# The last image's last queries in three blocks, and its last two involution units in parts ordered by row

## The chip, the cores and the metric

The kernel runs on one core of one Trainium2 chip. The metric is device time in microseconds (us), as the median of several runs; before the change it is 2607.41 us.

## The reference

The input is four images of 512 channels and 64x64 pixels, float32. Two layers follow each other:

- Attention. With N = 4096 pixels and 128 inner channels, `q`, `k` and `v` are 1x1 convolutions of `x`; `out[:, i] = sum_j v[:, j] * softmax_j(q_i . k_j)`; a 1x1 convolution `wo` brings it back to 512 channels, and `x` is added.
- Involution. `o1 = relu(W1 x)` has 128 channels in 8 groups of 16. For each pixel a small network (`Wr`, relu, `Ws`) makes 7x7 weights per group, `w[g, dy, dx]`. The output at a pixel is the sum over the 49 neighbours of `w[g, dy, dx] * o1[c, y + dy - 3, x + dx - 3]`, with zeros outside of the image. A 1x1 convolution `W3` brings it back to 512 channels, and the layer's input is added.

## The kernel before

**Attention.** The images go one after the other (`b`), the queries of an image in chunks of 512 pixels, that is eight rows (`c`, 0 to 7). `attention` runs steps: a step makes the scores of one block of queries against 128 keys (`pss`), ScalarE takes their exponential (`pt`), TensorE multiplies by `v` into `po`, and VectorE adds `pt` into `pacc`, whose last addition is `sums`. A block has `n` queries; with fewer than 512, one `pss` tile of 512 columns holds `512/n` keys' blocks. In the last image the last chunk is two blocks of 256 (blocks 7 and 8, here the image's rows 56 to 59 and 60 to 63).

**Finishing a block** (`finish_block`): `sums` is reduced (`blocks`), multiplied by `quads` (`pl`), inverted (`rls`), spread to all partitions (`spread`), multiplied into `on`; then `pwo` (four matmuls with additions into `x` on VectorE), `p1`, the relu `o1`, a transpose `pp`, a copy `o1t`, a DMA to a padded image `pix` in DRAM, and `pr` with its relu `red`, from which the taps' weights come.

**Involution.** A unit `u` is four image rows (16 units an image). It lies as two tiles `t` of 128 pixels, two rows each. `weights` makes `pw` (2 x 392 columns of PSUM) from `red`. The rows with their seven shifted windows are loaded from `pix` to `ring`, which has 12 slots for rows (`pump`, on SyncE's queue, three rows a piece at most in the last image). A VectorE instruction multiplies `n` values of `dy` for one shift `x` and both tiles: `prod <- ring, pw`, with 2 x `n` x 128 elements in a partition. `dy` goes in (0..3) and (4..6), cut into two where the rows would wrap in the ring. The products are summed over `x` and `dy` by GpSimd (`acc <- acc, prod`) and, in the tail, every second one by TensorE, with the product as stationary matrix and an identity as moving one (`pa`). `prods` has four buffers, so a product waits for the summing of the one four before it.

**Closing a unit** (`turn_unit`, `close_chunk`): TensorE adds `acc` to `pa`, ScalarE copies it (`accT`), and four matmuls `py` with four VectorE additions and the output DMA follow.

**Order.** Python generators are interleaved while the program is written: attention's steps drive, and `chores` steps the finishing, the closing and the products (`taps`), the latter by a planner's own times (`pe`, `free`, `due`). After the last attention step comes the tail: `tail` is set, the planner's waits fall away, a second PSUM pool for `pw` takes the place of the scores' (`wpools` then holds two, used in turn), and the loop steps finishing, closing and taps in turn until all is done. Within an engine's queue the order of the built program stands.

When a unit of the tail reaches `dy` 4, the kernel also makes the next unit's weights ahead:

```
                if o and dy >= DYS[1][0] > ops[o - 1][1]:
                    low = base + UR
                    pump()
                    if tail and units:
                        early[units[0]] = weights(*units[0])
...
            pw = early.pop((b, u), None) or weights(b, u)
```

The lines of the profile: products L356, GpSimd's sums L380, every matmul through `mm` L220 (told apart by tile), `sums` L699, `blocks` L537, the additions after `pwo` L560, after `py` L461, `pp` L590, `accT` L446, the ring's loads L257.

Of the kernel before, what the change touches and what calls it, by code (L numbers as in the profile page):

```python
# [8 lines left out]
F32 = mybir.dt.float32  # L9
AF = mybir.ActivationFunctionType  # L10
ALU = mybir.AluOpType
AX = mybir.AxisListType

B, C, H, W = 4, 512, 64, 64
N = H * W
P = 128
CT = C // P
CH = 512
NCH = N // CH
# [4 lines left out]
K = 7  # L24
PAD = 3
NTAP = K * K
GC = 16
G = P // GC
# [8 lines left out]
O_WP = 6 * 512  # L37
# [10 lines left out]
V_SP, V_BP = V_BVC + 1, V_BVC + 2  # L48
NVEC = V_BVC + 3

UR = 4
NT = UR // 2
NU = H // UR
# [3 lines left out]
RING = 12  # L57
STEP = 72
SR = UR + K - 2

DYS = (0, 4), (4, 3)
TAPS_A_US = 1.56


# [19 lines left out]
def fast_path(  # L84
# [91 lines left out]
    def takes(engine, us):  # L176
        free[engine] = max(free[engine], pe) + us
        return free[engine]
# [33 lines left out]
    def w_slice(off, t):  # L212
        return wt[:, off + t * P : off + (t + 1) * P]

    def v1(i):
        return vec[:, i : i + 1]

    def mm(o, lhsT, rhs, start=True, stop=True, shared=1):
        pe_us(rhs.free_size() * PE_COLUMN / shared)
        return nc.tensor.matmul(o, lhsT=lhsT, rhs=rhs, start=start, stop=stop)  # L220
# [19 lines left out]
    def pump():  # L240

        nonlocal load
        while load // STEP in written:
            b, row = divmod(load, STEP)
            rows, us = written[b]

            end = H + SR - UR if rows == H else rows + PAD - 1
            n = min(b * STEP + end, low + RING) - load
            n = min(n, RING - load % RING, PIECE if b == B - 1 else RING)
            if n <= 0:  # L250
                break
            for h in range(2):
                src = pix[b % 2][row + h : row + h + n, :W, :]
                windows = bass.AP(
                    tensor=src.tensor, offset=src.offset, ap=[[P, W], [WP * P, n], [1, K * P]]
                )
                nc.sync.dma_start(  # L257
                    ring[h * W : (h + 1) * W, load % RING : load % RING + n]
                    .rearrange("p r x c -> p r (x c)"),
                    windows,  # L260
                )
            free["dma"] = max(free["dma"], us)
            us = takes("dma", ROW_US * n) + LAND_US
            landing.update((load + i, us) for i in range(n))
            load += n
            if row + n == H + SR - UR:
                load = (b + 1) * STEP
# [4 lines left out]
        pace()  # L272


    def weights(b, u):
        red, col = reds[b, u]
        wpools.append(wpools.pop(0))
        pw = wpools[0].tile([P, NT, CH], F32, tag="w", name=f"pw_{b}_{u}")
        for t in range(NT):

            rows = slice(t * (P // NT), t * (P // NT) + CR + 1)
            pixels = slice(col, col + P)
            mm(
                pw[:, t, : NTAP * G], red[rows, pixels], wt[rows, O_WT : O_WT + NTAP * G],
                shared=2,
            )
        return pw
# [15 lines left out]
        nc.vector.tensor_scalar(verdict, pn, P - 0.5, None, ALU.is_lt)  # L303


    def involution():
        nonlocal low, due
        while True:
            while not units:
                yield "none"  # L310
            b, u = units.pop(0)
            acc = work2.tile([P, NT, 4, P], F32, tag="acc", name=f"acc_{b}_{u}")
            yield from until(free["dve"] + 0.3)
            pw = early.pop((b, u), None) or weights(b, u)
            begin = pe + 0.5
            pa, ops = None, []
            base = b * STEP + u * UR
            for dy0, n in DYS:

                at = (base + dy0) % RING  # L320
                whole = at + n + NT < RING + 1
                pieces = [(dy0, n)] if whole else [(dy0, 2), (dy0 + 2, n - 2)]
                ops += [(x, dy, k) for x in range(K) for dy, k in pieces]
            for o, (x, dy, n) in enumerate(ops):
# [5 lines that stand above are left out]
                rows = [(base + dy + t * 2) % RING for t in range(NT)]  # L330
                while base + dy + n + NT > load:
                    yield "wait"
                landed = max(landing[base + dy + i] for i in range(n + NT))
                while not tail and (
                    pe < max(begin, landed)
                    or free["dve"] > pe + (4.5 if b == B - 1 else 3.5)
                    or free["pool"] > pe + lag
                ):
                    yield "wait"
                free["pool"] = max(free["pool"], takes("dve", DVE_TAPS[0] + DVE_TAPS[1] * n))  # L340
                takes("pool", POOL_TAPS[0] + POOL_TAPS[1] * n)
                due -= n
                d0 = dy - DYS[dy >= DYS[1][0]][0]
                first = x == 0 and dy < DYS[1][0]
                prod, p0 = acc, d0
                if not first:
                    prod, p0 = prods.tile(
                        [P, NT, 4, P], F32, tag="prod", name=f"prod_{b}_{u}_{o}"
                    ), 0
                col = (x * K + dy) * G  # L350
                lines = ring[:, rows[0] : rows[0] + n, x, :]
                image = bass.AP(
                    tensor=lines.tensor, offset=lines.offset,
                    ap=[lines.ap[0], [(rows[1] - rows[0]) * K * P, NT], [K * P, n], [1, P]],
                )
                product = nc.vector.tensor_tensor(  # L356
                    prod[:, :, p0 : p0 + n, :].rearrange("p t d (g c) -> p t d g c", g=G),
                    image.rearrange("p t d (g c) -> p t d g c", g=G),
                    pw[:, :, col : col + n * G].unsqueeze(3)
                    .broadcast_to([P, NT, n * G, GC])  # L360
                    .rearrange("p t (d g) c -> p t d g c", d=n),
                    ALU.mult,
                )
                if not tail:
                    tc.keep_in_program_order(product)
                if first:
                    pass
                elif tail and o % 2:

                    begun = pa is not None  # L370
                    if not begun:
                        pa = ps1.tile([P, NT, P], F32, tag=("po", "acc")[u % 2], name=f"pa_{b}_{u}")
                    for t in range(NT):
                        for d in range(n):
                            mm(
                                pa[:, t, :], prod[:, t, d, :], ident,
                                not begun and t == d == 0, False,
                            )
                else:
                    nc.gpsimd.tensor_tensor(  # L380
                        acc[:, :, d0 : d0 + n, :], acc[:, :, d0 : d0 + n, :], prod[:, :, :n, :],
                        ALU.add,
                    )
                yield
            low = max(low, (b + 1) * STEP if u == NU - 1 else base + UR)
            pump()
            if pa is None:
                for n in (2, 1):
                    nc.gpsimd.tensor_tensor(  # L389
                        acc[:, :, :n, :], acc[:, :, :n, :], acc[:, :, n : 2 * n, :], ALU.add  # L390
                    )
            closing.append(turn_unit(b, u, acc, pa, takes("pool", POOL_OP * 1.5)))
# [127 lines left out]
    def finish_block(b, c, off, n, po, sums):  # L520
# [97 lines left out]
                    )  # L618
        us = takes("dma", PIX_US) + LAND_US

        pr = ps.tile([P, CH // NT], F32, tag="mm", name=f"pr_{name}")[:, : n // NT]
        for t in range(NT):
            half = slice(t * (P // NT), (t + 1) * (P // NT))
            mm(
                pr[half], w_slice(O_WP, 0)[:, half],
                o1.rearrange("p (u t x) -> p u t x", t=NT, x=P)[:, :, t, :], shared=2,
            )
        red = redpool.tile([P, CH // NT], F32, tag="red", name=f"red_{name}")[:, : n // NT]
        nc.scalar.activation(red, pr, AF.Relu, bias=v1(V_BP), scale=v1(V_SP))
        for i in range(tiles // NT):  # L630
            reds[b, top // UR + i] = red, i * P

        rows = top + n // W
        written[b] = rows, us
# [12 lines left out]
    def attention(b, kt, vT, q):  # L647
        blocks = [(c, 0, CH) for c in range(NCH)]
        if b == B - 1:

            blocks[-1:] = [(NCH - 1, off, CH // 2) for off in (0, CH // 2)]

        steps = [(k, j) for k, (_, _, n) in enumerate(blocks) for j in range(N // P * n // CH)]
        qs, pts, pos, paccs = {}, {}, {}, {}
# [470 lines left out]
```

## Time and profile before

| what | value |
|---|---|
| runs | 2607.64, 2607.41, 2604.98 us; median 2607.41 us |
| profiled execution, first to last instruction | 2605.7 us |
| median less the profiled span | 1.7 us |
| TensorE busy | 2587.9 us (99%) |
| VectorE busy | 1874.2 us (72%) |
| GpSimd busy | 1823.5 us (70%) |
| ScalarE busy | 835.8 us (32%) |
| mean granted TensorE clock | 0.997 |
| last exponential of the attention (`pt`) starts | 2522.82 us |

No other time of the profiled execution is given than its span; the median stands 1.7 us above it, for what lies around the instructions and for the spread of the runs. Start and duration in a line of the trace are microseconds from the span's start. A bracket behind a line of the timeline is the idle time of that engine before it, and what ended it. TensorE's rows count two instructions for one float32 matmul.

### The profile page before, as it was taken

What the parts mean: (1) busy time and instruction counts of PE and PEld (TensorE: products, weight loads), DVE (VectorE), ACT (ScalarE), POOL (GpSimd) and SP (SyncE); (2) the same over time, 40 slices, a digit from 0 to 9 for tenths busy, and PEclk for the clock granted to TensorE, in tenths of its full rate; (3) what the DMA queues carried; (4) which work ended last, traced back from release to release, by engine and by line L of the source; (5) the groups of instructions that cost most, each with busy time, mean ns of one, the idle gap of its engine ahead of it and who ended that gap; (6) DMA issues with size and microseconds to landing.
All of it is one profiled execution on the core that took longest, in us unless ns stands there. A gap on an engine that the chain in (4) does not pass through costs nothing.

```text
span 2605.7 us, 24569 instructions
## 1 busy us (share of the span) xinstructions
PE 2587.9 (99%) x7484; PEld 1246.5 (48%) x7484; DVE 1874.2 (72%) x2677; ACT 835.8 (32%) x1378; POOL 1823.5 (70%) x1197
## 2 busy tenths in 40 slices
PE   9999999999999999999999999999999999999998
PEld 7444444445544444444644444444464444444577
DVE  0447777877575787788676678788757678777887
ACT  1333333332233333333223333333323333333330
POOL 0007788877881788887885468888788577877886
PEclk9999999999999999999999999999999999999999
DMA  6033232445615344233651434443463433222343
GB/s 236 1 75 63 55 85 73 99 99 150 164 43 112 63 101 95 61 84 82 180 129 45 103 69 101 101 92 74 118 171 83 101 93 93 72 60 58 73 91 102
DMA packets 208798, 244.33 MB, mean 94 GB/s; under 512 B 109640, under 2 KB 128528, under 8 KB 208528
## 3 DMA queue, kind: packets, MB, share of 16 engines
q1 hardware_dynamic: 208224, 242.31, 38.6%
q8 instruction: 61, 1.00, 0.2%
q14 instruction: 81, 0.66, 0.1%
q10 hardware_dynamic: 432, 0.36, 0.0%
HBM read 193.57 MB, written 49.06 MB: 93 GB/s over the span
## 4 chain that ended last, share of the span: by engine, by line
PE 91%; POOL 4%; DVE 3%; issue 1%; DMA 0%; ACT 0%; SPq 0%; POOLq 0%; DVEq 0%; ACTq 0%
PE pss L220 32%; PE po L220 31%; PE pv L220 4%; PE pk L220 4%; PE pq L220 4%; PE pwo L220 4%; PE py L220 4%; PE p L220 4%; POOL acc L380 4%; PE pw L220 2%; DVE prod L356 1%; PE pa L220 1%; DVE pacc L696 1%; PE pr L220 1%; POOL acc L389 0%
## 5 line engine op out<-in xcount | busy, mean ns | idle before, releaser
L380 POOL TENSOR_TENSOR acc<-acc,prod 128x768 f32<-128x768 f32 (+3 forms) x1063 | 1701.5, 1620 | 760.5 <-DVE prod L356 712.4
L220 PE MATMUL pss<-q,k 128*128 128x512 f32 (+1 forms) x2112 | 1056.3, 585 | 0.0
L220 PE MATMUL po<-pt,v 128*128 128x512 f32 (+1 forms) x2112 | 1047.7, 581 | 0.0
L665 ACT ACTIVATE pt<-pss 128x512 f32<-128x512 f32 x1024 | 611.3, 597 | 1252.0 <-PE pss L220 1184.9
L356 DVE TENSOR_TENSOR prod<-ring,pw 128x512 f32<-128x512 f32 (+3 forms) x1092 | 886.7, 847 | 44.6 <-POOL acc L380 41.7
L696 DVE TENSOR_TENSOR pacc<-pacc,pt 128x512 f32<-128x512 f32 x958 | 664.6, 694 | 243.2 <-ACT pt L665 216.2
L220 PEld LDWEIGHTS po<-pt,v 128*128 128x128 f32 x2112 | 399.3, 190 | 482.2 <-issue 462.2
L220 PEld LDWEIGHTS pss<-q,k 128*128 128x128 f32 x2112 | 391.9, 190 | 466.2 <-issue 459.3
L404 DVE STREAM_TRANSPOSE turned<-acc 128x256 f32<-128x256 f32 x48 | 21.4, 446 | 217.4 <-POOL acc L389 217.4
L220 PE MATMUL py<-accT,wt 128*128 128x512 f32 (+1 forms) x264 | 132.3, 584 | 4.0 <-DVE x L461 3.3
L220 PE MATMUL pwo<-on,wt 128*128 128x512 f32 (+1 forms) x264 | 130.3, 586 | 0.0
L220 PEld LDWEIGHTS pv<-wt,x 128*128 128x128 f32 x1024 | 119.6, 192 | 15.3 <-issue 15.0
L389 POOL TENSOR_TENSOR acc<-acc 128x512 f32<-128x512 f32 x120 | 119.5, 996 | 9.4
L461 DVE SCALAR_TENSOR_TENSOR x<-py,vec,x 128x512 f32<-128x512 f32 (+1 forms) x132 | 95.7, 726 | 36.1 <-PE py L220 35.8
L220 PE MATMUL pv<-wt,x 128*128 128x128 f32 x1024 | 120.2, 275 | 0.0
L220 PE MATMUL p<-x,wt 128*128 128x512 f32 (+1 forms) x264 | 119.2, 579 | 0.0
L578 ACT ACTIVATE x<-x,vec 128x512 f32<-128x512 f32 (+1 forms) x132 | 92.9, 706 | 80.0 <-PE p L220 74.9
L220 PE MATMUL pk<-x,wt 128*128 128x512 f32 x256 | 117.3, 596 | 0.1
L220 PE MATMUL pq<-x,wt 128*128 128x512 f32 (+1 forms) x264 | 115.4, 580 | 0.0
L560 DVE SCALAR_TENSOR_TENSOR x<-pwo,bo,x 128x512 f32<-128x512 f32 (+1 forms) x132 | 95.2, 727 | 22.8 <-PE pwo L220 21.7
L356 DVE TENSOR_TENSOR acc<-ring,pw 128x1024 f32<-128x1024 f32 (+1 forms) x84 | 78.7, 955 | 17.6 <-PE pw L220 17.6
L220 PEld LDWEIGHTS pq<-x,wt 128*128 128x128 f32 x264 | 50.0, 190 | 60.2 <-issue 56.7
(57 smaller groups left out, 733.6 us busy)
## 6 DMA issues: line engine op xcount, KB each, us to landing
x<-x_dram SPq DMA_DIRECT2D x55, 1024.0 KB, 5.7
ring<-pix SPq DMA_DIRECT2D x74, 448.0 KB, 8.3
ring<-pix SPq DMA_DIRECT2D x24, 1344.0 KB, 9.7
out_dram<-x SPq DMA_DIRECT2D x31, 1024.0 KB, 4.2
ring<-pix SPq DMA_DIRECT2D x24, 896.0 KB, 10.7
ring<-pix SPq DMA_DIRECT2D x30, 672.0 KB, 10.2
ring<-pix SPq DMA_DIRECT2D x6, 2240.0 KB, 19.5
pix<-o1t SPq DMA_DIRECT2D x192, 32.0 KB, 1.7
```

The costliest lines, as they stand in the source:

```text
L220: return nc.tensor.matmul(o, lhsT=lhsT, rhs=rhs, start=start, stop=stop)
L356: product = nc.vector.tensor_tensor(prod[:, :, p0 : p0 + n, :].rearrange("p t d (g c) -> p t d g c", g=G), image.rearrange("p t d (g c) -> ...
L380: nc.gpsimd.tensor_tensor(acc[:, :, d0 : d0 + n, :], acc[:, :, d0 : d0 + n, :], prod[:, :, :n, :], ALU.add,)
L389: nc.gpsimd.tensor_tensor(acc[:, :, :n, :], acc[:, :, :n, :], acc[:, :, n : 2 * n, :], ALU.add)
L404: nc.vector.transpose(blocks.rearrange("p (t k q) -> p t k q", t=NT, q=TB), acc[:, :, 0, :].rearrange("p t (k q) -> p t k q", q=TB),)
L461: nc.vector.scalar_tensor_tensor(xt[:, t, :], py, v1(V_S3 + t), xt[:, t, :], ALU.mult, ALU.add)
L560: nc.vector.scalar_tensor_tensor(xt[:, t, :], pw, bo[:, t : t + 1], xt[:, t, :], ALU.add, ALU.add)
L578: nc.scalar.activation(xt[:, t, :], xt[:, t, :], AF.Identity, bias=v1(V_B3 + t))
L665: nc.scalar.activation(pt, pss, AF.Exp)
L696: nc.vector.tensor_tensor(paccs[k], paccs[k], pt, ALU.add)
```

## The change

- The last chunk of the last image is three blocks, of 256, 128 and 128 queries.
- The last two units (14 and 15 of image 3) are written by `last_units`, in nine parts of the list `LAST`. A part is (unit, tiles, first `dy`, how many `dy`); each part has seven products, one for each `x`. The order follows the rows that a part needs. Parts of unit 15 come in the tail only.
- Products that read only rows of padding are left out (unit 15, tile 1, `dy` 5 and 6), and the two last rows of the ring's loads with them.
- A block of one tile makes `pr` and `red` for one half of the partitions only; `reds` is kept by tile, and `weights` can make one tile's weights.
- `last_units` calls `weights` itself; it does not look into `early`. In unit 13 the call that fills `early` stays.

```diff
+PADDED = 2
+LAST = (
+    (0, (0, 1), 0, 2), (0, (0, 1), 2, 2),
+    (0, (0, 1), 4, 2), (0, (0,), 6, 1), (1, (0,), 0, 4),
+    (0, (1,), 6, 1), (1, (1,), 0, 4), (1, (0, 1), 4, 1), (1, (0,), 5, 2),
+)
...
-            end = H + SR - UR if rows == H else rows + PAD - 1
+            end = H + SR - UR - PADDED * (b == B - 1) if rows == H else rows + PAD - 1
...
-    def weights(b, u):
+    def weights(b, u, tiles=range(NT), pw=None):
+        if pw is None:
+            wpools.append(wpools.pop(0))
+            pw = wpools[0].tile([P, NT, CH], F32, tag="w", name=f"pw_{b}_{u}")
+        for t in tiles:
...
+    def last_units(b, u0):
...
+        for i, (v, tiles, dy, n) in enumerate(LAST):
+            u = u0 + v
+            while v and not tail:
+                yield "wait"
+            base = b * STEP + u * UR
+            while base + dy + 2 * tiles[-1] + n > load:
+                yield "wait"
...
+            fresh = [t for t in tiles if (v, t) not in weighed]
+            if fresh:
+                pws[v] = weights(b, u, fresh, pws[v])
+                weighed.update((v, t) for t in fresh)
...
+            for x in range(K):
+                while not tail and (
+                    pe < max(begin, landed)
+                    or free["dve"] > pe + 4.5
+                    or free["pool"] > pe + lag
+                ):
+                    yield "wait"
...
+                pas[v] = multiply_add(
+                    b, u, accs[v], pas[v], pws[v], tiles, x, dy, n, f"{i}_{x}",
+                    x == 0 and dy < DYS[1][0], bool(tail) and (x + i) % 2,
+                )
+                yield
+            if ends[v] == i:
+                closing.append(turn_unit(b, u, accs[v], pas[v], takes("pool", POOL_OP * 1.5)))
+        units.clear()
...
     def involution():
...
             b, u = units.pop(0)
+            if b == B - 1 and u == NU - 2:
+                yield from last_units(b, u)
+                return
...
-            blocks[-1:] = [(NCH - 1, off, CH // 2) for off in (0, CH // 2)]
+            blocks[-1:] = [(NCH - 1, 0, 2 * P), (NCH - 1, 2 * P, P), (NCH - 1, 3 * P, P)]
```

`multiply_add` is the body of the products' loop of before as a function: one product, summed by TensorE where its last argument is true, else by GpSimd, over the tiles of the part.

More of the change, by code (lines that the diff above doesn't have):

```diff
@@ L272, in chores @@
         pace()
-    def weights(b, u):
[L276 to L279, printed above, removed]
+    def weights(b, u, tiles=range(NT), pw=None):
[3 more added lines that the diff above has]
+        for t in tiles:
+            red, col = reds[b, u * NT + t]
             rows = slice(t * (P // NT), t * (P // NT) + CR + 1)
@@ L303, in tell, with multiply_add @@
         nc.vector.tensor_scalar(verdict, pn, P - 0.5, None, ALU.is_lt)
+    def multiply_add(b, u, acc, pa, pw, tiles, x, dy, n, o, first, by_pe):
+        base = b * STEP + u * UR
+        ts = slice(tiles[0], tiles[-1] + 1)
+        nt = len(tiles)
+        rows = [(base + dy + t * 2) % RING for t in tiles]
+        d0 = dy - DYS[dy >= DYS[1][0]][0]
+        prod, p0 = acc, d0
+        if not first:
+            prod, p0 = prods.tile([P, NT, 4, P], F32, tag="prod", name=f"prod_{b}_{u}_{o}"), 0
+        col = (x * K + dy) * G
+        lines = ring[:, rows[0] : rows[0] + n, x, :]
+        image = bass.AP(
+            tensor=lines.tensor, offset=lines.offset,
+            ap=[lines.ap[0], [(rows[-1] - rows[0]) * K * P, nt], [K * P, n], [1, P]],
+        )
+        product = nc.vector.tensor_tensor(
+            prod[:, ts, p0 : p0 + n, :].rearrange("p t d (g c) -> p t d g c", g=G),
+            image.rearrange("p t d (g c) -> p t d g c", g=G),
+            pw[:, ts, col : col + n * G].unsqueeze(3)
+            .broadcast_to([P, nt, n * G, GC])
+            .rearrange("p t (d g) c -> p t d g c", d=n),
+            ALU.mult,
+        )
+        if not tail:
+            tc.keep_in_program_order(product)
+        if first:
+            pass
+        elif by_pe:
+            begun = pa is not None
+            if not begun:
+                pa = ps1.tile([P, NT, P], F32, tag=("po", "acc")[u % 2], name=f"pa_{b}_{u}")
+            for t in tiles:
+                for d in range(n):
+                    mm(
+                        pa[:, t, :], prod[:, t, d, :], ident,
+                        not begun and t == tiles[0] and d == 0, False,
+                    )
+        else:
+            nc.gpsimd.tensor_tensor(
+                acc[:, ts, d0 : d0 + n, :], acc[:, ts, d0 : d0 + n, :], prod[:, ts, :n, :],
+                ALU.add,
+            )
+        return pa
@@ new lines, in last_units @@
+    def last_units(b, u0):
+        nonlocal low, due
+        accs, pas, pws, weighed = {}, {}, {}, set()
+        ends = {}
+        for i, part in enumerate(LAST):
+            ends[part[0]] = i
+        for i, (v, tiles, dy, n) in enumerate(LAST):
+            u = u0 + v
+            while v and not tail:
+                yield "wait"
+            base = b * STEP + u * UR
+            while base + dy + 2 * tiles[-1] + n > load:
+                yield "wait"
+            if v not in accs:
+                accs[v] = work2.tile([P, NT, 4, P], F32, tag="acc", name=f"acc_{b}_{u}")
+                pas[v], pws[v] = None, None
+            fresh = [t for t in tiles if (v, t) not in weighed]
+            if fresh:
+                pws[v] = weights(b, u, fresh, pws[v])
+                weighed.update((v, t) for t in fresh)
+            begin = pe + 0.5
+            landed = max(landing[base + dy + 2 * t + k] for t in tiles for k in range(n))
+            cost = len(tiles) * n / NT
+            for x in range(K):
[5 more added lines that the diff above has]
+                    yield "wait"
+                free["pool"] = max(free["pool"], takes("dve", DVE_TAPS[0] + DVE_TAPS[1] * cost))
+                takes("pool", POOL_TAPS[0] + POOL_TAPS[1] * cost)
+                due -= cost
+                pas[v] = multiply_add(
+                    b, u, accs[v], pas[v], pws[v], tiles, x, dy, n, f"{i}_{x}",
+                    x == 0 and dy < DYS[1][0], bool(tail) and (x + i) % 2,
+                )
+                yield
+            if ends[v] == i:
+                closing.append(turn_unit(b, u, accs[v], pas[v], takes("pool", POOL_OP * 1.5)))
+        units.clear()
@@ L342, in involution @@
                 due -= n
-                d0 = dy - DYS[dy >= DYS[1][0]][0]
                 first = x == 0 and dy < DYS[1][0]
[L345 to L383, printed above, removed]
+                by_pe = bool(tail) and o % 2
+                pa = multiply_add(b, u, acc, pa, pw, (0, 1), x, dy, n, o, first, by_pe)
                 yield
@@ L619, in finish_block @@
         us = takes("dma", PIX_US) + LAND_US
-        pr = ps.tile([P, CH // NT], F32, tag="mm", name=f"pr_{name}")[:, : n // NT]
-        for t in range(NT):
+        pr = ps.tile([P, CH // NT], F32, tag="mm", name=f"pr_{name}")[:, : max(n // NT, P)]
+        first = top // 2
+        whole = tiles > 1
+        for t in range(NT) if whole else [first % NT]:
             half = slice(t * (P // NT), (t + 1) * (P // NT))
[L624 to L631, printed above, removed]
+            pixels = o1
+            if whole:
+                pixels = o1.rearrange("p (u t x) -> p u t x", t=NT, x=P)[:, :, t, :]
+            mm(pr[half], w_slice(O_WP, 0)[:, half], pixels, shared=2 if whole else 1)
+        red = redpool.tile([P, CH // NT], F32, tag="red", name=f"red_{name}")[:, : max(n // NT, P)]
+        filled = slice(0, P) if whole else half
+        nc.scalar.activation(
+            red[filled], pr[filled], AF.Relu,
+            bias=v1(V_BP)[filled], scale=v1(V_SP)[filled],
+        )
+        for i in range(tiles):
+            reds[b, first + i] = red, i // NT * P
         rows = top + n // W
```

## The prediction

> **What bounds the kernel now.** First the page's busy times in 40 slices and its chain that ended last: TensorE is full from beginning to end.
>
> ```profile
> PE   9999999999999999999999999999999999999998
> ...
> PE 91%; POOL 4%; DVE 3%; issue 1%; DMA 0%; ACT 0%; SPq 0%; POOLq 0%; DVEq 0%; ACTq 0%
> ```
>
> So while attention runs, every added TensorE microsecond counts. In the built order of both programs each engine's rows are the same up to the last chunk of image 3, so only the last 110 us can move. There the chain (start, duration, what) leaves TensorE:
>
> ```profile
> 2522.82 0.61 ACT pt L665
> ...
> 2523.45 0.70 DVE sums L699
> ...
> 2525.52 1.67 DVE prod L356 x2
> ...
> 2545.96 2.37 POOL acc L380
> ...
> 2593.32 3.41 PE pa L220 x28
> ...
> 2599.81 0.48 DVE x L461
> ```
>
> No DMA stands in it. The busy times by stretch (columns: length, then PE, PEld, DVE, ACT, POOL with counts, granted clock, DMA share, GB/s), from the end of `sums` (I call it S, 2524.15) to the end of unit 13, and from there to the last product:
>
> ```profile
> 2524.15:2559.70 35.55, 31.51 (x200) 26.58 (x199) 30.87 (x48) 3.86 (x9) 25.27 (x16) 0.90 0.55 126
> 2559.70:2593.28 33.58, 31.61 (x229) 26.87 (x227) 31.80 (x42) 0.74 (x2) 27.16 (x18) 1.00 0.22 66
> ```
>
> VectorE works 30.87 + 31.80 = 62.67 us of 69.13 and TensorE 63.12: the tail is two nearly full engines, each waiting for the other in turn. VectorE's waits in it (us in total, times, longest):
>
> ```profile
> DVE x L560 <- PE pwo L220: 2.2, 4, 0.8
> DVE prod L356 <- POOL acc L380: 1.9, 4, 0.8
> DVE x L461 <- PE py L220: 1.4, 2, 1.0
> DVE prod L356 <- PE pa L220: 0.8, 2, 0.4
> ```
>
> None is for a ring row. The last ring load was issued at 2568.3, loads land in 6.9 us at the median (2575.2), and unit 15's first product ran at 2577.50 without idle time: rows have a margin of 2.3 us. Durations come from the groups by form (the last two numbers before the idle time are busy us and mean ns of one):
>
> ```profile
> L356 DVE TENSOR_TENSOR prod<-ring,pw 128x512 f32<-128x512 f32 x33 | 21.3, 678 | 0.8 <-POOL acc L380 0.8
> ...
> L356 DVE TENSOR_TENSOR prod<-ring,pw 128x256 f32<-128x256 f32 x10 | 4.1, 414 | 1.1 <-POOL acc L380 1.1
> ...
> L461 DVE SCALAR_TENSOR_TENSOR x<-py,vec,x 128x256 f32<-128x256 f32 x8 | 3.8, 480 | 4.3 <-PE py L220 4.3
> ```
>
> and from the timeline:
>
> ```profile
> 2560.29 4.86 DVE L356 TENSOR_TENSOR prod<-ring,pw 128x512 f32<-128x512 f32 x8
> ```
>
> Eight products of 512 in 4.86 us are 0.607 from start to start, 0.07 below the mean of one (678 ns). Likewise 1.15 for 1024 and 0.87 for 768 (four in 4.60, the next start 3.45 after four). With the same 0.07 off, 256 costs 0.34; 128 lies, on the line through 678 and 414 ns, at 282 ns, so 0.21 (no row shows it: not above 0.34, the 256; not below 0.07).
>
> **One: the attention ends later.** From block 7's step 13 on, the built orders have the same matmuls up to the last `pss` but for these. (a) 29 groups of `pss` and `po` are four 128x128 matmuls instead of two 128x256. A group of 256 takes 0.864; 32 instructions of 128 (`pv`) took 3.57, so eight take 0.893: 29 x 0.029 = 0.84. (b) `pl` of the second block comes inside attention: four matmuls, and two took 0.34 at 2498.69: 0.68. (c) One `py` of 512 now stands before the last `pss`: 0.86. Sum 2.4. Then VectorE: an addition after that `py` and product 12_5 (unit 12, sixth) now stand ahead of `sums`. The `py` ends 0.89 before the last `pss`; 0.67 + 1.15 makes 1.82, against 0.89 + 0.65 for the exponential: 0.3 late. S moves by **+2.7** (bounds 1.5, where the order hides (c), to 3.7).
>
> **Two: what VectorE has to do after S.** 12_5 and one addition of 512 are now ahead of S: -1.15 - 0.67. `spread` and `on` of the last block have half the width: -0.26. Eight additions of 128 after `pwo` instead of four of 256: one is 0.40 start to start and 0.27 on the line to 128: 8 x 0.27 - 4 x 0.40 = +0.56. Units 14 and 15: before 14 x 0.607 + 14 x 0.87 + 7 x 1.15 = 28.7; after 35 x 0.607 + 14 x 0.34 + 14 x 0.21 = 28.9, so +0.2: the padding saved is 7 x 256 of 7 x 3584 elements, and 28 further instructions eat it. Two more additions after `py` stand before the last product: +0.8. Sum **-0.5**.
>
> [...]
>
> **Three: where VectorE waits after S.** I followed the queues with these durations, TensorE at 0.111 per instruction of `pa` (16 in 1.78), GpSimd at 1.285 for 512, 0.733 for 256, 0.46 for 128.
> - `py` after attention: TensorE still has 3.55 of `po` and `pwo` after its last `pss`, then half of `pw` (0.85) and the `py` (0.86), ready at S+3.65; VectorE is there at S+2.85: 0.8.
> - `pl` of the last block comes behind `pa`, ready 0.5 late. `pwo` then finds other products ahead of it: before's 2.2 is gone.
> - Unit 13, products 9 to 13, four buffers behind GpSimd and TensorE: 1.2. Its last product ends at S+30.85.
> - Unit 14's start is new. Its weights are made early, as before, but `last_units` makes them **again**, in the pool where unit 13's lie, so the pair waits for unit 13's last product and for what TensorE has queued. From S+13.1 TensorE has hardly a gap: 52 `pa` matmuls of unit 13's products (11.5), 8 that close unit 12 (1.8), `pw` 14 in two halves (1.7), `p1` (0.9), `pp`, `pr`, `pn` (0.5), half of `pw` 15 (0.85) and what is left of unit 12 (0.9), then the pair (0.93): the weights come at S+33.3. VectorE idles 2.5. If TensorE were not behind, it would be 0.93 + hand-offs = 1.1.
> - Units 14 and 15: a GpSimd sum of 512 takes longer (1.285) than the two products per sum (1.21), the small parts come behind a full buffer ring, and unit 15's second half waits for its weights: 2.5, against 1.78 before.
> - Each of about eight products let go by TensorE costs its drain, 0.15 (16 instructions are busy 1.95 and start to start 1.80): 1.2.
>
> Sum 8.7, against 69.13 - 62.67 = 6.46: **+2.2**.
>
> **Four: the end.** Before, 28 instructions (3.41) follow the last product. After, its sum is GpSimd's (0.07 + 0.73 + 0.1 behind the sum before) and 16 instructions follow (1.85): 2.75, **-0.7**. From there to the end nothing differs (copy, four `py`, four additions, output DMA). Off the path: the additional DMAs. Unit 13's later rows and the last three rows stand behind the verdict's load in SyncE's queue in the new order; that is at S+21, the rows need the slots that unit 13 gives back at S+23 anyway, land about 7 later, and part 6 first needs them at about S+55: cover 25 us, cost nothing. TensorE sums units 14 and 15 with 164 instructions instead of 180, 1.8 us less, which is already in the waits of part three.
>
> **The sum.** 2.7 - 0.5 + 2.2 - 0.7 = +3.7: span 2605.7 + 3.7 = 2609.4, and 1.7 around it, so 2611.1 against the median 2607.41. Within 0.2% (5.2 us, about what a measurement of this kernel can tell from no change).
>
> **Rivals.**
> - *The TensorE clock drops in the stretch S+13 to S+33.* Slower. Before, a TensorE gap of 3.30 us up to 2531.59 was followed by this (chain, then the stretch, whose granted clock is 0.66):
>
> ```profile
> 2531.59 1.19 PE pa L220 x4
> 2532.79 1.71 PE pwo L220 x4
> ```
>
> ```profile
> 2530.00:2540.00 10.00, 8.40 (x34) 7.17 (x34) 7.26 (x13) 0.45 (x2) 8.44 (x5) 0.66 0.34 76
> ```
>
> Four `pwo` took 1.71 instead of 0.86. In the new order the widest gap, behind `pl`, is 1.15, after which TensorE is the bound. Ten microseconds at 0.66 would cost 3.4: 2614.5. [...] Small pieces that occupy VectorE like the 256 ones (14 x 0.13) or GpSimd (6 x 0.27) push to the same side: 2613 to 2615.
> - *TensorE is less behind than I have it*, so the second pair costs 1.1 and the drains nothing, and S moves by 1.5 only: -1.4 - 1.2 - 1.2: 2607.3.
> - *Rows were what the tail waited for*, so that earlier rows free it: the waits view has no such wait, and the built order puts no product of unit 14 ahead of attention's last `sums`, before or after. Even with every VectorE wait gone: 2.7 - 0.5 - 0.7 - 6.46 = -5.0: 2602.4, hardly over the bound.
>
> **The numbers.** My case 0.60 (2608.5 to 2614; one in five above 2612.6, the bound); the slower rival 0.21 (to 2616.5); the less late TensorE 0.15; all waits gone 0.04. Faster 0.04; slower 0.21 + 0.12 = 0.33; same 0.63. From 2605 to 2616.5 leaves under 2 in 10 out.
>
> **What would show it.** Right: `sums` of the last block ends near 2526.9; between unit 13's last product and unit 14's first, VectorE idles 1 to 3 us, released by `pw`; no idle time from a ring load; products of 128 near 0.28. Wrong: no `pw` wait, a granted clock under 0.9 behind S+13, or a last product before S+66 of the new S.

## The result and the profile after

| | before | changed kernel |
|---|---|---|
| median of ten runs | 2606.59 us | 2612.18 us |
| lowest to highest | 2604.80 to 2607.88 | 2611.68 to 2615.21 |
| profiled span | 2605.7 us | 2610.2 us |

The ratio is 1.0023 (95% interval 1.0014 to 1.0032): slower by 5.6 us, just outside of the 0.2% that a measurement of this kernel can tell. Forecast were 2611.1 us, slower by 3.7, inside that bound; the range of 2605.0 to 2616.5 holds the result.

One thing has to be set right before traces are compared. Up to `pq` of the last chunk all programs with four buffers issue the same instructions, yet the transposes `pp` of block 6 of image 3, which come just ahead of it, start at 2475.51 us in the profile before and at 2474.18 in the one after; over nine such profiles they start between 2473.80 and 2476.92. So I count from there (point A). From A to the end of the span it is 130.19 us before and 136.02 after (the span is read to a tenth): +5.83, which is near the 5.6 of the medians.

The two stretches of the tail in the changed kernel (columns as in the prediction), from what follows the last `sums` to the end of unit 13, and from unit 14's first product to the end of the last one:

```profile
2525.47:2557.84 32.37, 31.17 (x222) 25.78 (x221) 27.91 (x49) 5.33 (x16) 23.33 (x15) 1.00 0.57 137
2560.58:2597.60 37.02, 32.91 (x212) 27.07 (x213) 33.72 (x71) 0.75 (x2) 26.98 (x28) 0.95 0.12 43
```

Between the two lie 2.74 us that are in neither. The waits view of the same time shows them, and what else VectorE waits for:

```profile
DVE acc L329 <- PE pw L227: 2.7, 1, 2.7
DVE prod L329 <- PE pa L227: 2.5, 5, 1.1
DVE prod L329 <- POOL acc L353: 2.0, 5, 0.8
DVE x L523 <- PE py L227: 1.3, 2, 1.1
DVE verdict L311 <- PE pn L309: 1.2, 1, 1.2
DVE rls L608 <- PE pl L227: 0.5, 1, 0.5
```

Before's 2.2 for `pwo` is gone; the first line is new, and no line names a ring load. The chain shows the place of the new wait: half of unit 15's `pw`, a sum, the second pair for unit 14, and only then unit 14's first product.

```profile
2557.73 0.85 PE pw L227 x2
2558.58 1.09 PE pa L227 x8
2559.67 0.88 PE pw L227 x4
2560.55 0.02 issue
2560.58 0.69 DVE acc L329
```

The groups by form, mean ns after the busy time, for the shapes of the parts; the 128 one is new:

```profile
L329 DVE TENSOR_TENSOR prod<-ring,pw 128x512 f32<-128x512 f32 x38 | 24.1, 684 | 1.6 <-PE pa L227 1.3 <-POOL acc L353 0.3
...
L329 DVE TENSOR_TENSOR prod<-ring,pw 128x256 f32<-128x256 f32 x21 | 8.2, 415 | 0.9 <-POOL acc L353 0.6 <-PE pa L227 0.2
...
L329 DVE TENSOR_TENSOR prod<-ring,pw 128x128 f32<-128x128 f32 x14 | 3.4, 285 | 2.0 <-POOL acc L353 1.0 <-PE pa L227 0.9
```

Last the end of the chain, behind the last product (2597.60):

```profile
2597.21 0.43 POOL acc L353
2597.64 0.34 issue
2597.98 0.50 POOLq L1105
2598.48 0.27 POOL acc L353
2598.75 0.04 issue
2598.79 1.84 PE pa L227 x14
```

L1105 is the load of the verdict, which GpSimd's queue holds too. In the chain it seems to stand ahead of the very last sum, with 0.84 us. GpSimd's own timeline shows that it takes nothing there:

```profile
2596.41 2.33 POOL L353 TENSOR_TENSOR acc<-acc,prod 128x256 f32<-128x256 f32 x3 [1.34 <-DVE prod L329]
```

The last three sums run in 2.33 us, some 0.73 each and under 0.1 between two of them; the load runs beside the last one. That sum waits for the one before it, which ends 0.34 us after the last product.

The 0.95 in the second line of the tail's stretches is the granted clock. It is not spread over the stretch: from 2581 to 2583 us it is 0.50, and it falls while TensorE sums products of unit 15.

```profile
2580.00:2585.00 5.00, 5.00 (x26) 4.50 (x26) 3.84 (x10) 0.00 (x0) 4.22 (x4) 0.66 0.00 0
2579.85 4.54 PE L227 MATMUL pa<-ident,prod 128*128 128x128 f32 x24 [0.80 <-DVE prod L329]
```

At the prediction's 0.111 us each, 24 instructions take 2.7 us.

### The profile page after: what moved, and what is told of

It reads as the page before. It is cut to its first block, busy times and chain, and to the rows that moved or that the text cites. A ratio compares the mean times of both kernels' runs of the same rounds, so it can differ in the third digit from the quotient of the medians.

```text
span 2610.2 us, 24936 instructions
## 1 busy us (share of the span) xinstructions
PE 2592.1 (99%) x7636; PEld 1252.4 (48%) x7636; DVE 1875.9 (72%) x2713; ACT 837.6 (32%) x1387; POOL 1823.0 (70%) x1210
## 4 chain that ended last, share of the span: by engine, by line
PE 90%; POOL 4%; DVE 4%; issue 1%; ACT 0%; POOLq 0%; DVEq 0%; ACTq 0%
PE pss L227 31%; PE po L227 31%; PE pv L227 4%; PE pk L227 4%; PE pq L227 4%; POOL acc L353 4%; PE p L227 4%; PE pwo L227 4%; PE py L227 4%; PE pw L227 2%; DVE prod L329 2%; PE pa L227 1%; DVE pacc L764 1%; PE pr L227 1%; POOL acc L451 0%
## 5 line engine op out<-in xcount | busy, mean ns | idle before, releaser
L227 PE MATMUL pss<-q,k 128*128 128x512 f32 (+2 forms) x2176 | 1055.8, 572 | 0.0
L227 PE MATMUL po<-pt,v 128*128 128x512 f32 (+2 forms) x2176 | 1047.9, 568 | 0.0
L329 DVE TENSOR_TENSOR prod<-ring,pw 128x512 f32<-128x512 f32 (+4 forms) x1119 | 889.5, 831 | 46.6 <-POOL acc L353 42.1
L227 PE MATMUL pwo<-on,wt 128*128 128x512 f32 (+2 forms) x272 | 129.0, 567 | 0.0
L227 PE MATMUL p<-x,wt 128*128 128x512 f32 (+2 forms) x272 | 119.5, 568 | 0.0
L640 ACT ACTIVATE x<-x,vec 128x512 f32<-128x512 f32 (+2 forms) x136 | 93.8, 693 | 79.2 <-PE p L227 74.1
L227 PE MATMUL pq<-x,wt 128*128 128x512 f32 (+2 forms) x272 | 115.6, 568 | 0.0
L622 DVE SCALAR_TENSOR_TENSOR x<-pwo,bo,x 128x512 f32<-128x512 f32 (+2 forms) x136 | 96.0, 714 | 20.6 <-PE pwo L227 19.4
```

The source lines that it names most:

```text
L329: product = nc.vector.tensor_tensor(prod[:, ts, p0 : p0 + n, :].rearrange("p t d (g c) -> p t d g c", g=G), image.rearrange("p t d (g c) - ...
L622: nc.vector.scalar_tensor_tensor(xt[:, t, :], pw, bo[:, t : t + 1], xt[:, t, :], ALU.add, ALU.add)
L640: nc.scalar.activation(xt[:, t, :], xt[:, t, :], AF.Identity, bias=v1(V_B3 + t))
```

## The experiments

All are compared with the kernel before, whose median in the three batches was 2606.53, 2606.60 and 2606.38 us (33 runs each); each experiment has 11 runs. A to end is from one profile each; the profiled execution of e1, e7 and e11 was the slowest of its eleven.

| run | products in units 14, 15 | median us | ratio and interval | A to end us |
|---|---|---|---|---|
| changed kernel | 63 | 2612.18 | 1.0023 (1.0014 to 1.0032) | 136.02 |
| e1_use_early | 63 | 2611.50 | 1.0019 (1.0010 to 1.0028) | 135.58 |
| e2_blocks_only | 35 | 2605.91 | 0.9998 (0.9989 to 1.0007) | 129.88 |
| e3_parts_only | 63 | 2612.00 | 1.0021 (1.0012 to 1.0031) | 135.09 |
| e4_coarse_two_blocks | 42 | 2606.07 | 0.9996 (0.9987 to 1.0005) | 129.00 |
| e5_last_by_pe | 63 | 2612.06 | 1.0022 (1.0013 to 1.0031) | 135.40 |
| e6_six_buffers | 63 | 2607.52 | 1.0003 (0.9994 to 1.0012) | 132.41 |
| e7_coarse_three_blocks | 42 | 2606.41 | 0.9999 (0.9990 to 1.0008) | 131.11 |
| e8_seven_parts | 49 | 2608.90 | 1.0009 (1.0000 to 1.0018) | 131.50 |
| e9_before_six | 35 | 2602.03 | 0.9981 (0.9972 to 0.9990) | 127.83 |
| e10_coarse_two_six | 42 | 2602.23 | 0.9984 (0.9975 to 0.9993) | 127.66 |
| e11_coarse_three_six | 42 | 2605.07 | 0.9992 (0.9983 to 1.0001) | 130.88 |
| e12_change_six | 63 | 2608.40 | 1.0008 (0.9999 to 1.0017) | 134.54 |

**The two halves of the change, each alone.**

```diff
 # e2_blocks_only: the changed kernel without its units in parts
-PADDED = 2
+PADDED = 0
...
-            if b == B - 1 and u == NU - 2:
-                yield from last_units(b, u)
-                return
```

> The three blocks alone: units 14 and 15 as before the change, with the products of padding. Theory (the blocks cost TensorE time while attention runs, and no product waits for a row): the last sums come 2.6 us later against the last chunk's start, about 1 us of it is won back after it because work has moved ahead, so 2607.5 to 2609.5. Rival (rows that come earlier free the tail): the time is that of before, 2606.6, or below it.

```diff
 # e3_parts_only: the changed kernel with the blocks of before
-            blocks[-1:] = [(NCH - 1, 0, 2 * P), (NCH - 1, 2 * P, P), (NCH - 1, 3 * P, P)]
+            blocks[-1:] = [(NCH - 1, off, CH // 2) for off in (0, CH // 2)]
```

> The parts alone: two blocks of 256 queries as before the change, units 14 and 15 in the nine parts and without padding. Theory (the second pair of weights costs about 2.7 us, the small parts about as much as the padding saves or up to 2 us more, the last sum on GpSimd under 1 us): 2608.5 to 2611. Rival (the parts gain and only the blocks lose): under 2606.

The parts alone are as slow as the whole change (2612.00), the blocks alone as fast as the kernel before (2605.91). Both theories had numbers between the two. That the blocks would cost nothing I had not expected: the time is the rival's, but not for the rival's reason. The profile of e2_blocks_only says how: its last `sums` end 51.37 us behind A, as in the changed kernel (51.38), against 48.63 before, so 2.74 us are paid; but unit 14 begins 83.58 us behind A, and in the kernel before unit 13 ends there too (2559.70, less 0.6 for a product of unit 14 that ran ahead, is 83.6 behind A). Everything is won back in between. One thing that differs there is the clock: before, a TensorE gap of 3.30 us is followed by a granted clock of 0.50 from 2531 to 2537 us, while in e2_blocks_only the gap in that place is 1.12 us and the clock stays at 1.00. How much of the 2.74 us this is was not separated. The two stretches of e2_blocks_only:

```profile
2526.41:2558.70 32.29, 31.09 (x222) 25.79 (x221) 27.83 (x50) 5.33 (x16) 23.37 (x15) 1.00 0.60 141
2558.70:2592.37 33.67, 30.95 (x228) 26.49 (x227) 32.16 (x43) 0.75 (x2) 27.10 (x17) 1.00 0.21 64
```

The first line has the numbers of the changed kernel's first line, the second has 33.67 us where the changed kernel has 37.02. So the loss lies wholly behind unit 13, in the 2.74 us of waiting for weights and in units 14 and 15. That rows were awaited is refuted as far as these runs go: e2_blocks_only brings the rows earlier and gains nothing that the measurement can tell.

**The second pair of weights.**

```diff
 # e1_use_early: unit 14 takes the weights that were made ahead
-                pas[v], pws[v] = None, None
+                pas[v], pws[v] = None, early.pop((b, u), None)
+                if pws[v] is not None:
+                    weighed.update((v, t) for t in range(NT))
```

> The change with one edit: last_units takes unit 14's weights from those made ahead (early) instead of making them a second time. Theory (the wait is for the second pair, which has to wait for unit 13's last product): VectorE's 2.73 us idle before unit 14's first product fall under 0.5, TensorE does 0.93 us less, and the time falls by 2 to 3 us from 2612.2 to about 2609.5. Rival (TensorE's queue is what is late there, whichever weights stand in it): VectorE goes on at once but stops four products later on TensorE, and the time falls by 0.9 at most, to 2611.3.

The wait for `pw` before unit 14 is gone from its profile, but the time is lower by only 0.7 us, and from A to the end by 0.44. By the medians my theory that 2 to 3 us come back fails, and the rival's size is the measured one. Two things in the profile stand against the 2.73 us. First, unit 13 ends 1.2 us later there, though TensorE's order is the same as in the changed kernel up to that point. The same twelve instructions behind the gap at `pl`, in the changed kernel and in e1, and e1's granted clock just behind (third number from the end):

```profile
2536.99 1.60 PE L227 MATMUL pa<-ident,prod 128*128 128x128 f32 x12 [1.12 <-DVE prod L329]
2539.73 2.33 PE L227 MATMUL pa<-ident,prod 128*128 128x128 f32 x12 [1.11 <-DVE prod L329]
2541.00:2543.00 2.00, 2.00 (x11) 2.00 (x11) 1.21 (x3) 0.00 (x0) 1.71 (x1) 0.50 1.06 274
```

In e7_coarse_three_blocks the clock falls in the same place and unit 13 ends 84.86 us behind A, as in e1 (84.87); in e2, e8 and the changed kernel it does not fall, and unit 13 ends 83.58 to 83.66 behind A. So this 1.2 us belongs to that execution's clock and not to the edit. Whether e1's other executions had it is not known; the fastest of them took 2609.80 us, the fastest of the changed kernel 2611.68. What taking the weights once is worth therefore stays between 0.4 and some 2 us. Second, units 14 and 15 take 38.11 us instead of 37.02, at full clock and with these waits:

```profile
DVE prod L329 <- POOL acc L353: 2.8, 7, 0.8
DVE x L525 <- PE py L227: 0.9, 2, 0.6
DVE prod L329 <- PE pa L227: 0.2, 1, 0.2
```

This 1.1 us of the stall was turned into other waits: products that start earlier wait for GpSimd's sums later (2.8 us here, 1.7 in units 14 and 15 of the changed kernel).

**Fewer, larger products.**

```diff
 # e4_coarse_two_blocks: blocks of before, weights made once, and
-    (0, (0, 1), 0, 2), (0, (0, 1), 2, 2),
-    (0, (0, 1), 4, 2), (0, (0,), 6, 1), (1, (0,), 0, 4),
-    (0, (1,), 6, 1), (1, (1,), 0, 4), (1, (0, 1), 4, 1), (1, (0,), 5, 2),
+    (0, (0, 1), 0, 2), (0, (0, 1), 2, 2), (0, (0, 1), 4, 3),
+    (1, (0, 1), 0, 4), (1, (0, 1), 4, 1), (1, (0,), 5, 2),
 # e7_coarse_three_blocks: the same with the blocks of the change
 # e8_seven_parts: e7 with the third part cut in two
-(0, (0, 1), 4, 3),
+(0, (0, 1), 4, 2), (0, (0, 1), 6, 1),
```

> Two blocks of 256 as before the change, weights made ahead are used, and coarse parts: unit 14 as 2, 2 and 3 values of dy for both tiles, unit 15 as 4 and 1 for both tiles and 2 for the first tile; no products of padding. 42 products instead of 35 before and 63 in the change. Theory (leaving the padding out is worth 7 x 256 of 7 x 3584 elements, less 7 further instructions of 0.07, and the same share of the summing): VectorE -1.3 us, time 2604.5 to 2606. Rival (the end is set by the closing chain and hand-offs, so saved products are free anyway): 2606.6, no change.

> The change with the coarse parts of e4_coarse_two_blocks (42 products instead of 63, no padding) and unit 14's weights made once, with the three blocks of the change. Theory (the loss lies in the number of small parts; the blocks alone were 2605.9 against 2606.5 and give back after the attention what they take in it): 2604.5 to 2606.5, as e4_coarse_two_blocks or a little better. Rival (blocks and parts hinder each other, so that the three blocks cost where the units are in parts): 2608 to 2610.

> Three blocks, unit 14's weights made once, and seven parts: unit 14 as 2, 2, 2 and 1 values of dy, unit 15 as 4 and 1 values and 2 for the first tile, both tiles together everywhere else; 49 products, no padding. Between e7 (42 products) and e1_use_early (63 products, 2611.5). Theory (each further product costs about the same): a quarter to a third of the way from e7 to e1_use_early, 2606.5 to 2607.5. Rival (only the parts of a single tile cost): as e7.

With three blocks and weights made once there are four kernels that do these units in 35 (e2, padding included), 42, 49 and 63 products: 2605.91, 2606.41, 2608.90 and 2611.50 us. The time rises with the number, 5.6 us for 28 products, some 0.2 us each. e8 came 1.4 us above the upper end that I had for it. The medians hold what differs ahead of unit 14 too. From unit 14's first product to the end of the last one, at full clock in all four profiles, it is 33.67 us (e2, shown above) and, for e7, e8 and e1:

```profile
2561.05:2595.52 34.47, 31.13 (x216) 26.15 (x215) 31.87 (x51) 0.74 (x2) 27.08 (x21) 1.00 0.13 47
2559.20:2594.71 35.51, 32.92 (x222) 27.14 (x222) 32.36 (x58) 0.74 (x2) 26.68 (x23) 1.00 0.13 46
2561.79:2599.90 38.11, 33.84 (x222) 27.18 (x222) 33.91 (x72) 0.74 (x2) 27.72 (x29) 1.00 0.12 42
```

That is 4.4 us for 28 products, 0.16 us each; VectorE's work grows by 1.75 us of it, the rest is waiting. The number is not alone in these steps (e1 also splits by tile and takes another order), so that the count is the cause is a reading of a row of four, not a separate proof. Leaving the padding out is worth little: e4 has 0.9996 with an interval that holds 1, and from A to the end it is 1.2 us below the kernel before.

**The last sum.**

```diff
 # e5_last_by_pe
-                    x == 0 and dy < DYS[1][0], bool(tail) and (x + i) % 2,
+                    x == 0 and dy < DYS[1][0], bool(tail) and (x + i + (i == len(LAST) - 1)) % 2,
```

> The change with one edit: in the last part every second product is the other engine's, so that the very last product is summed by TensorE as it was before the change. Theory (after the last product the trace shows 12.6 us to the end, of it 0.73 of GpSimd's last sum and 0.84 around a load of the verdict that stands in GpSimd's queue ahead of it): that stretch falls to about 11.8 us and the time by 0.7 to 1.2 us, 2611 to 2611.5. Rival (the queue of sums ends at the same time whoever takes the last): no change, 2612.2.

From the last product to the end it is 11.9 us instead of 12.6, but only 0.5 of this is the sums: TensorE's last one ends 2.6 us behind the last product instead of 3.0. The other 0.3 lies behind the last addition, where both programs are the same. The 0.84 us for the load was my misreading of the chain, as shown above. The median differs by 0.1 us from the changed kernel's, which the runs cannot resolve, so the time does not confirm a gain.

**Buffers.**

```diff
 # e6_six_buffers: e1_use_early with
 # e9_before_six: the kernel before with
 # e10_coarse_two_six: e4 with; e11_coarse_three_six: e7 with; e12_change_six: the changed kernel with
-    prods = pool("prods", 4)
+    prods = pool("prods", 6)
```

> The change with unit 14's weights made once (as in e1_use_early, 2611.5) and six buffers for products instead of four. Theory A (small products turn over the four buffers faster than GpSimd and TensorE hand them back, so the loss of the parts is waiting on buffers): VectorE's waits for GpSimd and TensorE, 4.4 us in e1_use_early, fall under 2, and the time falls by 2 to 3 us, to 2608.5 to 2609.5. Theory B (the loss is the work itself: more instructions on every engine, each with its fixed share): waits move but the time stays within 1 us of 2611.5.

> The kernel before with six buffers for products instead of four, nothing else. Control for e6_six_buffers. Theory (the four buffers bind most where products are small; the kernel before has 1.9 us of waits for GpSimd in unit 13 and 0.8 for TensorE): under 2 us gained, 2605 to 2606.5. Rival (six buffers are worth the 4 us of e6_six_buffers everywhere, whatever the parts): 2602.5 to 2603.5.

> e4_coarse_two_blocks (two blocks, coarse parts, no padding, weights made once; 2606.1) with six buffers: the version meant to beat both kernels. Theory (its 3.6 us of waits for GpSimd and TensorE in the tail become shorter by the buffers, but the finishing chain and the closing chain stay): 2603.5 to 2605.5. Rival (its waits are on the queue of sums itself, not on buffers): 2606.

> e7_coarse_three_blocks (2606.4) with six buffers. Theory: as e10_coarse_two_six within 1 us, since the blocks alone made no difference; 2604 to 2606. Rival (buffers help the three blocks more, because their finishing has more short steps): 2602 to 2603.5.

> The change as it is, with unit 14's weights made a second time, and six buffers. Together with e6_six_buffers (2607.5, weights made once) it prices the second pair where buffers do not hide it. Theory (with four buffers taking it out was worth 0.7 because the products then waited for sums; with six the wait of 2.7 us shows): 2609 to 2610.5. Rival (it is worth 0.7 here too): 2608.2.

e6 fell by 4.0 us, more than theory A had said, and alone it would have looked like its proof. The control refutes it: the kernel before gains as much (4.35 us, 0.9981), so four buffers are not what makes the parts slower than the kernel before. With six buffers, too, the change is 6.4 us slower than the kernel before (2608.40 against 2602.03). The five profiles with six buffers have point A at 2472.0 to 2472.7 instead of 2473.8 to 2476.9, so a part of the gain lies ahead of the change, over the whole attention: between the profiles of before and e9 it is 3.04 us ahead of A and 2.4 behind it. Some of the 3.04 is the clock: before has a granted clock of 0.83 in the ten microseconds from 380 us, e9 has no such drop ahead of A, and neither have the four-buffer profiles with A at 2473.8 to 2474.5. The waits of products for GpSimd's sums fall from 41.7 us to 10.0 over the whole of e9, while those of `turned` for GpSimd rise from 217.4 to 234.2. My expectation for e9 failed because I had looked at the tail only; e10 came below its range for the same reason.

With six buffers, the second pair of weights costs 0.9 us by the medians of e12 and e6, and 2.1 from A to the end; my figure of 2 to 3 holds by the second and not by the first. And the three blocks, which cost nothing in e2, cost 2.8 us between e10 and e11 (I had expected these within 1 us of each other). In e11's profile the granted clock falls to 0.50 from 2537 to 2539 us, and unit 14 begins 83.81 us behind A; in e6, without that drop, it begins at 82.53. So some 1.3 us of the difference can be the clock; the rest was not tried. e9 and e10 beat both kernels, by 4.3 and 4.2 us against before; padding left out makes no difference between them that can be told.

## Why the prediction was right, and where it was not

- *What bounds the tail* (two nearly full engines, no row awaited): right. VectorE is busy 27.91 + 33.72 us of the 72.13 from the last `sums` to the last product, TensorE 31.17 + 32.91 in the two stretches.
- *One, the attention ends later by 2.7.* Measured 51.38 - 48.63 = 2.74 (ends of `sums` behind A), with its parts (a) to (c) as the order gave them. What it did not say plainly is that this term and the better finishing behind it belong together: alone they cancel to nothing (e2). The sum had them with opposite signs, so its total did not suffer by that.
- *Two, VectorE's work.* The line through 678 and 414 ns gave 282 for 128 elements; 285 was measured. Units 14 and 15 have 33.72 us of VectorE where e2_blocks_only has 32.16, so +1.6 instead of +1.0 (+0.2 and +0.8). The eight products that gave 0.607 start every 0.60 us; the 0.607 holds the end of the last one, which makes 0.2 us over 35 products. In the same way those of 1024 start every 1.13 us and not every 1.15.
- *Three, the waits.* The first `py` waits 1.1 (0.8 expected), `pl` 0.52 (0.5), the second pair of weights 2.73 (2.5), `pwo`'s 2.2 is gone. Units 14 and 15 took 37.02 us; by the prediction's terms 33.2 of work (28.9 of products, 2.7 and 1.6 of additions), 2.5 and 1.2 of waits, so 36.9. What I missed is the verdict's wait for `pn`, 1.19, whose matmul stands behind others in TensorE's queue in the new order. With it, the time without work of VectorE from the last `sums` to the last product rose from 6.46 us to 10.50, so +4.0 where this term had +2.2. How much of the 2.5 for the weights would come back if they were made once is not settled: e1 gave 0.7 by the medians, with a clock drop in its profile. A part of the stall returned as other waits (1.1 us in units 14 and 15).
- *Four, the end.* Wrong in sign. Expected -0.7, measured +0.2 (12.60 against 12.43). From the last product to the end of TensorE's last sum it is 3.03 us against 3.45, so -0.4: GpSimd's last sum ends 1.1 us behind the last product, where I had 0.9, because the sum before it is late. From there to the end of the last addition it is 3.57 against 3.56. The remaining 0.6 lies behind the last addition, 6.0 us to the end of the span against 5.4, where I had said that nothing differs. Over the fourteen profiles this last piece runs from 5.4 to 6.0 us with the same instructions in it, so it is at least in part spread.
- *The rivals.* The TensorE gap behind `pl` was 1.12 us (1.15 expected), and the granted clock stayed at full in the ten microseconds around it:

```profile
2536.00:2546.00 10.00, 8.93 (x59) 7.04 (x60) 10.00 (x18) 2.34 (x7) 5.44 (x3) 1.00 0.70 177
```

  so in the stretch that it named, the slower rival did not come. But the sign that I had given for being wrong, a granted clock under 0.9 behind S+13, did come, 55 us behind S: 0.66 over the five microseconds from 2580, shown above, behind TensorE gaps of 0.81 and 0.80 us. It cost little. From the first product of unit 15's first tile to that of its second it is 6.86 us in the changed kernel and 6.58 in e1, which has the same parts and full clock there. In these traces the length of a gap alone does not decide whether the clock falls: 1.12 us here without a drop and 1.11 in e1 and e7 with one, and the drop in unit 15 came behind gaps of at most 0.81. The other signs were as forecast: `sums` ends at 2525.56, which is 2526.9 when counted from the A of before; the wait for `pw` is there, and no wait for a row. Rows as the bound fell with e2.
- *The sum.* +3.7 forecast, +5.6 measured, +5.8 behind A. Behind A the missing 2.1 us are about 1.8 in the waits of term three, of which the verdict's 1.2 was not in the sum at all, and 0.9 at the end, less 0.5 by which VectorE's work fell further than in term two (62.67 to 61.63). The likeliest case was one within 0.2%; the result lies just outside.

What stays open: why 63 small products with fewer elements in sum cost some 5 us more than 35. Their part is in VectorE's busy time (+1.6) and in waits for sums, of which e1 has 2.8 us and e2 0.6 on GpSimd; six buffers do not close the difference. Whether order or count decides the rest was not separated.

## What to carry to other kernels

Here an engine that hands small pieces to two others lost time as the pieces grew in number, even where they held fewer elements (units 14 and 15: 33.67 us in 35 products, 38.11 in 63): count instructions on every queue before cutting a step to start it earlier, and first look whether anything waits for what comes earlier. Removing a measured stall can be worth less than the stall, because something else is late next; here 1.1 us of 2.7 came back as other waits. Before a difference between two profiles is put down to an edit, compare the granted clock in short windows: one drop here moved a unit's end by 1.2 us in the same order of instructions. And a step of the chain needs a look at the engine's own timeline: the chain put a load ahead of GpSimd's last sum, and the timeline shows that the sum did not wait for it. And a control on the kernel before belongs to every experiment that frees a resource: six buffers looked like the cure of the change (4.0 us) and were a gain of their own (4.35 us without the change).

## What was not expected of the hardware

- The granted clock fell to 0.50 for some microseconds in the tails of twelve of the fourteen profiles while TensorE still had work, all but those of e2 and e8. Behind a TensorE gap of 3.30 or 3.31 us, as in all five kernels with two blocks, it fell each time. Behind the gap of 1.11 or 1.12 us of the nine with three blocks it fell in three (e1, e7, e11) and not in six.
- Programs with the same instructions reached the same point between 2473.8 and 2476.9 us, while from that point on, `sums` ended 48.63 us behind A in each of the five kernels with two blocks and 51.37 or 51.38 in each of the nine with three. What differs between runs came from ahead of that point, and goes with the clock. In windows of 10 us it is full ahead of A in three of the nine profiles with four buffers (the changed kernel, e4, e5: A at 2473.80 to 2474.50), falls once in five (before, e2, e3, e7, e8: 2475.12 to 2476.31) and twice in e1 (2476.92).
